# An attention layer over the whole graph: weights divided by their sums beforehand, features on the output's partitions, and one additive term moved to ScalarE

## The chip, the cores and the metric

The kernel runs on one core of a Trainium2 chip. The metric is the device time of one execution in microseconds (us); the runs below give its median and their spread. A profile of one further execution shows what each engine did: TensorE (PE, with its weight loads as PEld), VectorE (DVE), ScalarE (ACT), GpSimd (POOL) and SyncE (SP), which issues the DMAs.

## The reference, cut to what matters

The input x is 32 batches of 512 nodes with 256 features, in fp32. Four graph attention layers follow each other, each as `x = x + layer(relu(layernorm(x)))`. All but a part of the second use an adjacency matrix that is the same for every batch. The second layer holds the part that is changed, an attention over all nodes without a mask:

```python
out = relu(x @ mlp1_w + mlp1_b)            # 512 features
residual = out
h = out @ W_fc                             # relu(out) is out
f1 = h @ a[:F, 0]                          # one score per row i
f2 = h @ a[F:, 0]                          # one score per column j
e = leaky_relu(f1[:, :, None] + f2[:, None, :], 0.2)
out = elu(softmax(e, axis=2) @ h)
out = elu(out) + residual
out = relu(out @ mlp2_w + mlp2_b)          # then a masked attention follows
```

Because the exponential of a leaky rectifier is the larger of two exponentials, an unnormalized weight is the larger of two products, exp(s_i) exp(t_j) and exp(0.2 s_i) exp(0.2 t_j), each shifted by the row's highest score. No exponential over the full 512 x 512 matrix is needed, only products of columns and rows, and a maximum.

## The kernel before, in words

**Tiling.** The nodes of a batch are four tiles of 128 (NT = 4). Features are D = 256 (KD = 2 tiles) or F = 512 (KF = 4 tiles; HF = 256 is half of F). Everything is fp32, apart from masks and throw-away outputs in bf16. `transposes` (line 412) and `product` (line 422) issue all PE work; a product accumulates `nk` matmuls in one PSUM tile.

**Order.** The kernel does not issue work as it is written. Each call of `do` records a piece, with its engine, an estimated duration and the tiles that it reads and writes, in the graph of its batch. `Plan.order` then runs through all graphs, up to five batches being open at once (DEPTH, line 36): it gives each free engine the ready piece with the lowest key, if tiles of its kind are free (SLOTS, line 34). A key is the batch's start (a multiple of PERIOD, line 37) less an entry of the tables URGENCY or FIRST, with corrections for the first and last three batches (EARLY, LAST). Where the plan leaves a gap of 400 ns or more on PE, some filler transposes, `filled`, are put behind the piece (lines 303 to 309 and 1029 to 1031). The instructions stand on each engine in that order, and semaphores keep the dependencies. Tiles come from rings by size: b8 (7 tiles), b4 (14), b2 (14), b1 (10), and 7 PSUM tiles.

**The changed function, `full_gat_T` (lines 841 to 928).** It takes `srcT`, which is out1T, mlp1's output with features on partitions, and overwrites it.

1. The projection: for each half g of the features and each node tile, four matmuls of 257 columns give 256 features of h and one score column. ACT or DVE copies them to `hfc` with 1 added (lines 852 and 854), DVE copies the score (line 855), and POOL writes a column of ones ahead of the first half (line 856).
2. The scores: the highest t of all nodes is found by a reduction, a transpose (`row`, line 861) and another reduction. Then `c` gets four columns per node tile, and one exp of ACT turns them into the factors (lines 867 to 873).
3. The weights: the first factor becomes a row on all partitions by a transpose, a copy (`turned`), a DMA to a line in DRAM and a DMA that broadcasts it (`lines`, `row_of`); the second by four transposes (`spread`). For each node tile jt, ACT scales the one row (line 884) and DVE takes the larger of the two products (line 891) into `ptf`, with the summed-over node j on partitions.
4. The output: for each tile of output nodes and each half, four matmuls with `ptf` as the stationary operand give the numerators, and the first half's extra column gives the denominator. DVE inverts it. ACT applies exp with that scale (line 919), DVE clamps at 1 (line 921), ACT takes exp again (line 922), DVE takes the larger (line 923): the two elu's. The result `ef` has nodes on partitions; 16 transposes per batch bring it back to features on partitions (lines 924 to 926), where DVE adds the residual (line 928).

**The moved term, in `weights_T` (lines 697 to 738).** In two of the four masked attentions of a batch (`even`: after mlp2, and in the last layer), the weights are exp(y + g), where y is the larger of two sums (DVE, line 711) and g is the mask plus a column (POOL, line 717). POOL adds the two (line 721), ACT applies exp (line 722). In the others POOL adds the mask (line 729), and the column is the exp's bias (line 736).

SP issues all DMAs in one order: the batch's input and output, the lines (line 650) and the rows (line 658).

Of the kernel before, what the change touches and what calls it, by code (L numbers as in the profile page):

```python
# [12 lines left out]
AF = mybir.ActivationFunctionType  # L13
# [4 lines left out]
P = 128  # L18
# [18 lines left out]
PERIOD = 103600  # L37
# [7 lines left out]
    43943, 23247, 115444, 28195, 131913, 11021, 150223, 75332, 64495, 133886, 120583, -1101, 94222, 220028,  # L45
    153204, 195513, 90595, 143135, 39950, 165919, 68946, 151319, 9986, 99423, -64152, 52386, 56209, -25494,
    -12505, 125025, -53702, 14840, 134100, 44025, 75158, 8077, 5304, 34581, 45115, 207, -14505, -58518,
    -42176, 75304, -43249, 2933, -19079, -76505, 34586, 51948, 58461, 37338, 44003, -28740, 75374, -78348,
    112017, 44148, -58283, 98931, -23346, -97990, 220212, 87878, 79564, 158375, 51171, 129288, 201256,
    95579, 178029, 176359, -9875, 112826, 199490, -47172, 150423, 84738, 36922, 65744, 89892, 57714, -7531,  # L50
    116483, 40997, 60827, 84702, -240140, 134571, 84185, 72437, 26458, 201340, -116771, -2680, 101206,
    -132113, 11638, 71562, 75236, 19480, 46590, 3896, -69776, 176509, 41349, 41392, 177010, -34515, 59197,
    133037, 87352, 93705, 227861, -7065, 107008, 165322, 17092, 37203, 20572, -3112, 22963, -41216, 38751,
    -37768, 141292, 13106, 30339, 76908, -48735, -54474, 215553, -103644, -6626, 112885, -184359, 72027,
    51563, 88489, 3327, 65551, 105362, 20604, 16381, 36085, 32001, -99329, -107296, -77792, -14723, -136588,
    -100872, -76217, -76147, -259685, -382832, -98027, -197658, -65246, -109857, -125895, -128830, -71459,
    -54813, -57765, 69303, -25676, 10283, -57471, -91828, 79555, 144115, 97457, 180007, 275371, 122987,
    193691, -13364, -53043, -8290, -24035, -15402, -4875, 66615, -8638, -39945, -35041, -48603, -2815,
    -61303, 120173, 102541, 38375, 105200, -71290, -57098, 52007, 94397, -14845, 62753, -26544, -65371,
    -207649, -70898, -69840, -88366, 27159, 104701, 262750, 227584, 196761, 278139, 357683, 279755, 27422,  # L60
    248480, 108362, 230662, 134572, 115371, 155959, 149054, 138805, 77100, 101057, 158810, -88764, 168382,
    77636, 33563, 175809, 112632, 187077, 261718, 117631, 32335, 158631, 1036, -74122, -92596, -12280,
    -146905, 229, 30106, -218718, 7963, -350233, -180610, -79527, -130467, -138492, 17419, -363510, 17356,
    -87268, -271311, -121896, -287651, -76457, -87505, -107851, -318651, -60440, -314406, -66548, -86247,
    -83362, 109349, -288469, 59508, -50249, -21194, -109175, 16924, -42145, -115301, -73511, -299831,
    -68604, -275254, 28335, -37411, -32891, -86918, -129954, -102101, -103415, 21936, -114404, -114436,
    -145621, -54624, -37490, -6786, 226411, -26192, -6061, -25033, 89934, -63272, -82592, 17489, 114806,
    44461, -56264, -87386, -48407, -77170, -87670, -38020, -116914, -38471, -69348, -228506, -215782,
    -54813, -122090, -191577, -55569, -105209, -92182, 28921, -72616, -45523, -49012, -33598, -76273,
    -123170, -174959, 25865, -176706, -124610, -100893, 38989, -172406, -133057, -112099, -99070, -322085,  # L70
    -184282, -219066, -253145, -331833, -169829, -337339, -215940, -163206, -231858, -186736, -108690,
    -196995, -157932, -153450, -248828, -196863, -195477, -223174, -198595, -177361, -206813, -220380,
    -215473, -189492, -160863, -118730, -100154, -74131, 49765, -92141, -214916, -28639, -104791, -137597,
    -30328, -23299, -117546, -70645, -88590, -193216, -218783, -157264, -44754, -117265, -5302, 33583,
    -119484, -41578, 15533, -126430, -111215, -205150, -228722, -168637, -210347, -216720, -159680, -206661,
    -245080, -232690, -61360, -203052, -91590, -122985, -96910, -101903, -107874, -169770, -263511, -226800,
    -253496, -193433, -134757, -250170, -101415, -193028, -330813, -240582, -244977, -358942, -121881,
    -249516, -161367, -68855, -318842, -170307, 33948, -249896, -67102, 38118, -270429, -262193, -234703,
    -182336, -90808, -271458, -194411, -200974, -260557, -213451, -142575, -225302, -284934, -174965,
    -262450, -321002, -146122, -209826, -335580, -243074, -220269, -267185, -269236, -178724, -227851,  # L80
    -396486, -233722, -281737, -132057, -171227, -215236, -199050, -190642, -245900, -181074, -484732,
    -105243, -123637, -227989, -161274, -240673, -150119, -4587, -279569, -211555, -250700, -333147,
    -337122, -257764, -311553, -311455, -273568, -344195, -289986, -197478, -308673, -317223, -455899,
    -303145, -338677, -369201, -488187, -325862, -303656, -344479, -310759, -403328, -446498, -415994,
    -522626, -557538, -378731, -463941, -346054, -453692, -395203, -657915, -481677, -469324, -391813,
    -501282, -465541, -477163, -272939, -582288, -372007, -349639, -208955, -335296, -409233, -455808,
    -447653, -379056, -413166, -439115, -503757, -468515, -418430, -426118, -497159, -360337, -392505,
    -245697, -615652, -650803, -595281,
]
FIRST = [  # L90
    -36661, 19893, -21726, 135503, 85633, 237464, 129132, 171706, 120477, 219412, 125455, 134502, -84836,
    -139537, 39854, 172698, 159381, 199547, 210247, 61158, 103584, 167776, -20431, 3682, 26992, -43725,
    -40836, 27300, 147323, 97757, 40687, 56084, -29470, -69216, -165149, -232111, -89157, -106634, -114869,
    -16735, -130987, 24281, -83920, 52821, -168646, -55535, -145649, -62544, -83048, 6792, -15864, -31602,
    98655, -133287, -166750, -141261, -242450, -135463, -222160, -177245, -98591, -114406, -102410, -79761,
    -264672, -62129, -235867, -253085, -231089, -200529, 16618, -165024, -152414, -165668, 42901, -112970,
    -174603, -113382, -156161, -303346, -252928, -385439, -410003, -195151, -326551, -248605, -317343,
    -163957, -208536, -182534, -24101, -70360, -16833, -208324, -228344, -253210, -209178,
# [3 lines left out]
    [127714, 124300, 140109, 1275316, 20684, 3710, 30790, 20023],  # L102
    [21381, 1446513, 75479, -3218, 89835, 61799, 992, -5994],
    [16582, -743, 947951, -35616, 537487, -26713, 362315, 602],
]
LAST = [
    [136435, 122850, 411901, 1447410, 146100, 513359, -692128, 374735],
    [14763, 42474, 104030, 510068, 166538, -178446, 1731034, 221293],
    [5870, -6330, 13392, 2190, 30176, 62234, 471784, -1052314],
# [226 lines left out]
def gat_stack(  # L336
# [230 lines left out]
    WFC = fixed("wfc", [P, KF, 2, HF + 1])  # L567
# [3 lines left out]
    for s in range(2):  # L571
        for k in range(KF):
            fold(WFC[:, k, s, HF : HF + 1], WFC[:, k, :, :HF], row[:, s])
# [123 lines left out]
    def weights_T(ca, line_b, cc, ct, farT, even):  # L697
# [6 lines left out]
        for jt in range(NT):  # L704
# [8 lines left out]
            if even:  # L713
                g = Later("b2", "g", [P, N])

                def lifted(o, far, c, _):
                    return nc.gpsimd.tensor_scalar(o, far, 1.0, c, ALU.mult, ALU.add)  # L717


                do(POOL, 665, [g.all], [farT[:, jt, :], ct(jt), y.all], lifted)  # L720
# [120 lines left out]
    def full_gat_T(srcT):  # L841

        stt = nc.vector.scalar_tensor_tensor

        hfc = Later("b8", "hfc", [P, NT, 2, HF + 2])
        for g in range(2):
            for t, mm in project(srcT, lambda k: WFC[:, k, g, :], HF + 1, [hfc]):
                v = hfc[:, t, g, 1 : HF + 1]  # L850
                if t % 2 == 0:
                    do(ACT, 300, [v], [mm[:, :HF]], lambda o, a: nc.scalar.activation(o, a, AF.Copy, bias=1.0))
                else:
                    do(DVE, 335, [v], [mm[:, :HF]], lambda o, a: nc.vector.tensor_scalar(o, a, 1.0, None, ALU.add))
                do(DVE, 75, [hfc[:, t, g, HF + 1 :]], [mm[:, HF:]], nc.vector.tensor_copy)
# [21 lines left out]
        for jt in range(NT):  # L877
# [14 lines left out]
            )  # L892


        es = []
        for it in range(NT):
            e = Later("b2", "ef", [P, F])
            rden = Later("tiny", "rdenf", [P, 1])
# [185 lines left out]
```

## Time and profile before

| what | value |
| --- | --- |
| runs, median of 3 | 3432.81 us (3430.71 to 3441.22) |
| profiled execution | 3439.92 us, span of its instructions 3438.2 us |
| mean granted PE clock | 0.996 |
| PE, weight loads | 3400.9, 2852.8 us busy |
| DVE, ACT, POOL | 2678.3, 1965.3, 1640.6 us busy |
| DMA | 110.51 MB, 10.3% of the engines' time in the main queue |
| changed function's product, PE | 2048 records, 489.7 us busy |
| its projection, PE | 2048 records, 471.1 us busy |
| transposes of ef, PE | 512 records, 68.6 us busy |
| the term g, POOL | 256 instructions, 176.6 us busy |

Lines of a group read: source line, engine, operation, output and input tiles, shapes and count; then busy time in us, mean duration of one in ns, and the engine's idle time just before with what ended it. An instruction's row by tile gives shortest, median and longest duration in ns. Lines in order of time give start and duration in us. A wait reads: who waited for whom, us in total, times, longest. An fp32 matmul leaves two records in the profile, a transpose one. PE's records overlap, because a matmul's end is modelled: its busy time is no sum of its means.

### The profile page before, as it was taken

How to read it: one execution, taken by the hardware profiler on the slowest of the kernel's cores; microseconds unless marked ns; L12 is line 12 of the kernel's file. 1: busy time of each engine (PE TensorE's matmuls, PEld its weight loads, DVE VectorE, ACT ScalarE, POOL GpSimd, SP SyncE). 2: the span in 40 equal slices, each digit the busy share in tenths (PEclk: the TensorE clock that was granted, in tenths of full speed). 3: DMA queues.
4: the chain of work that ended last, by engine and by line, in shares of the span. 5: the costliest groups of instructions: out<-in, count | busy, mean ns of one | idle time of the engine just before them, and what ended most of it. 6: DMA issues, size and time to landing. Idle time of an engine off the chain costs nothing. (4 is left out here: it accounts for less than half of the span.)

```text
span 3438.2 us, 55054 instructions
## 1 busy us (share of the span) xinstructions
PE 3400.9 (99%) x18685; PEld 2852.8 (83%) x18685; DVE 2678.3 (78%) x8200; ACT 1965.3 (57%) x4109; POOL 1640.6 (48%) x2089
## 2 busy tenths in 40 slices
PE   8999999999999999999999999999999999999998
PEld 7788888888888888888888888888888888888887
DVE  8587778877878777878778788778788778878675
ACT  3555655665655656555656555656556565556554
POOL 3243544544544535444445445445445354445346
PEclk8999999999999999999999999999999999999999
DMA  3010110011110110100101100101101101001001
GB/s 111 16 32 11 37 38 23 25 35 32 38 38 11 38 35 32 38 26 22 38 28 38 38 26 22 35 32 38 38 12 36 35 32 38 26 22 41 16 23 38
DMA packets 77977, 110.51 MB, mean 32 GB/s; under 512 B 7168, under 2 KB 43520, under 8 KB 77696
## 3 DMA queue, kind: packets, MB, share of 16 engines
q1 hardware_dynamic: 77696, 106.98, 10.3%
q8 instruction: 149, 2.44, 0.3%
q14 instruction: 132, 1.08, 0.1%
HBM read 89.66 MB, written 17.30 MB: 31 GB/s over the span
## 5 line engine op out<-in xcount | busy, mean ns | idle before, releaser
L729 POOL TENSOR_TENSOR y<-y,farT_some 128x512 f32<-128x512 f32 x512 | 579.9, 1162 | 348.9 <-DVE y L711 336.8
L422 PE MATMUL mm<-v,pt 128*128 128x257 f32 x3072 | 704.5, 380 | 2.1 <-ACT pt L722 2.0
L711 DVE SCALAR_TENSOR_TENSOR y<-row,cc,rb 128x512 f32<-128x512 f32 x896 | 619.0, 742 | 59.5 <-DMA rb<-line 37.5
L422 PEld LDWEIGHTS mm<-v,pt 128*128 128x128 f32 x3072 | 573.6, 190 | 85.7 <-ACT pt L722 4.0
L736 ACT ACTIVATE pt<-y,ct 128x512 f32<-128x512 f32 x640 | 457.0, 719 | 171.7 <-POOL y L729 162.1
L422 PEld LDWEIGHTS mmh<-vh,pt 128*128 128x128 f32 x4096 | 489.2, 193 | 11.7 <-issue 1.9
L422 PE MATMUL mmh<-vh,pt 128*128 128x65 f32 x4096 | 485.3, 274 | 1.1 <-ACT pt L736 0.7
L422 PE MATMUL mm<-hfc,ptf 128*128 128x257 f32 (+1 forms) x2048 | 474.1, 381 | 1.2 <-DVE ptf L891 0.9
L422 PE MATMUL mm<-wfc,out1T 128*128 128x257 f32 x2048 | 471.1, 379 | 0.0
L668 DVE CUSTOM_DVE_ANT_0 left<-row,far_nz 128x512 bf16<-128x512 f32 x640 | 414.0, 681 | 64.5 <-PE row L412 64.2
L422 PEld LDWEIGHTS mm<-wfc,out1T 128*128 128x128 f32 x2048 | 382.2, 189 | 53.4
L422 PEld LDWEIGHTS mm<-hfc,ptf 128*128 128x128 f32 x2048 | 379.1, 190 | 52.8 <-POOL y L729 2.2
L721 POOL TENSOR_TENSOR y<-y,g 128x512 f32<-128x512 f32 x256 | 322.4, 1275 | 131.5 <-DVE y L711 116.9
L627 ACT ACTIVATE h<-xt,shift,rstd 128x256 f32<-128x256 f32 x512 | 274.6, 591 | 82.7 <-DVE shift L619 76.6
L612 POOL TENSOR_SCALAR rstd<-mv 128x4 f32<-128x4 f32 x128 | 35.1, 275 | 580.4 <-DVE mv L1028 537.9
L974 POOL TENSOR_TENSOR rz<-rz,res 128x256 f32<-128x256 f32 x128 | 93.7, 733 | 316.2 <-ACT rz L953 310.7
L953 ACT ACTIVATE ez<-mm,rden 128x256 f32<-128x256 f32 x256 | 119.1, 466 | 200.5 <-DVE rden L1028 197.5
L422 PE MATMUL mm<-hT,w 128*128 128x512 f32 x512 | 230.7, 593 | 0.0
L422 PE MATMUL mm<-out1T,wm 128*128 128x512 f32 x512 | 225.2, 592 | 0.0
L1028 DVE BATCH_NORM_STATS2 stats<-xt 128x6 f32<-128x256 f32 x512 | 201.9, 415 | 7.8 <-DMA xt<-in_x_dram 5.0
L668 DVE CUSTOM_DVE_ANT_0 left<-row,far_pos 128x512 bf16<-128x512 f32 x256 | 167.4, 685 | 41.2 <-PE row L412 41.2
L422 PEld LDWEIGHTS mm<-out1T,wm 128*128 128x128 f32 x512 | 95.0, 190 | 107.0 <-issue 99.7
(150 smaller groups left out, 5721.0 us busy)
## 6 DMA issues: line engine op xcount, KB each, us to landing
rb<-line SPq DMA_DIRECT2D x256, 256.0 KB
xt<-in_x_dram SPq DMA_DIRECT2D x32, 512.0 KB
out_dram<-xt SPq DMA_DIRECT2D x32, 512.0 KB
line<-turned SPq DMA_DIRECT2D x128, 2.0 KB
adj_sb<-in_adj_dram SPq DMA_DIRECT2D x1, 1024.0 KB
wfc<-in_L_gnn_W_fc_dram SPq DMA_DIRECT2D x2, 512.0 KB
a_row<-in_L_gnn_a_dram SPq DMA_DIRECT2D x3, 256.0 KB
a_row<-in_L_gnn_a_fc_dram SPq DMA_DIRECT2D x1, 512.0 KB
```

Source lines behind the costliest of these rows:

```text
L422: nc.tensor.matmul(o, lhsT=parts[k], rhs=parts[nk + k], start=(k == 0), stop=(k == nk - 1))
L612: do(POOL, 200, [rstd.all], [mv[:, :, 1]], lambda o, a: nc.gpsimd.tensor_scalar(o, a, EPS, None, ALU.add))
L627: lambda o, a, m, s: nc.scalar.activation(o, a, AF.Relu, bias=m, scale=s),
L668: return nc.vector.tensor_tensor_reduce(out=junk, in0=a, in1=far, scale=1.0, scalar=LOWEST, op0=ALU.add, op1=ALU.max, accum_out=o,)
L711: lambda o, a, c, b: nc.vector.scalar_tensor_tensor(o, a, c, b, ALU.add, ALU.max),
L721: do(POOL, 1255, [y.all], [y.all, g.all], lambda o, y, g: nc.gpsimd.tensor_tensor(o, y, g, ALU.add))
L729: lambda o, y, far: nc.gpsimd.tensor_tensor(o, y, far, ALU.add),
L736: lambda o, a, c: nc.scalar.activation(o, a, AF.Exp, bias=c),
L953: do(ACT, ns, [o.all], [z, scale], lambda o, a, s=scale, f=f: nc.scalar.activation(o, a, f, scale=s))
L974: do(POOL, 685, [r], [r, res[:, it, :]], lambda o, a, b: nc.gpsimd.tensor_tensor(o, a, b, ALU.add))
L1028: made = p.run(*(r.ap() if isinstance(r, Ref) else r for r in p.args))
```

## The change

In `full_gat_T`:

- both score columns are made in the first half of the projection (258 columns), the second has 256; the scores go to a small tile `stf`, and `hfc` has neither ones nor scores;
- the denominators are made before the weights: with output nodes on partitions, ACT scales a row (now the fourth factor), DVE takes the larger of two products and sums it in the same instruction (`accum_out`); the first two factors are multiplied by the inverse sums (`rq`);
- the weights `ptf` are then built as before, from rows and columns of `rq`, so that their sums are 1;
- the product has `hfc` as the stationary and `ptf` as the moving operand, 512 columns wide, with features on the output's partitions; the exps, clamp, maximum and residual follow on 512 columns, without transposes.

In `weights_T`, g is made by ACT (Identity with a bias). All tables of the plan and PERIOD are new.

```diff
-PERIOD = 103600
+PERIOD = 102900
...
-    WFC = fixed("wfc", [P, KF, 2, HF + 1])
+    WFC = fixed("wfc", [P, KF, 2, HF + 2])
...
-            fold(WFC[:, k, s, HF : HF + 1], WFC[:, k, :, :HF], row[:, s])
+            fold(WFC[:, k, 0, HF + s : HF + s + 1], WFC[:, k, :, :HF], row[:, s])
...
-                    return nc.gpsimd.tensor_scalar(o, far, 1.0, c, ALU.mult, ALU.add)
-                do(POOL, 665, [g.all], [farT[:, jt, :], ct(jt), y.all], lifted)
+                    return nc.scalar.activation(o, far, AF.Identity, bias=c)
+                do(ACT, 615, [g.all], [farT[:, jt, :], ct(jt), y.all], lifted)
...
-        hfc = Later("b8", "hfc", [P, NT, 2, HF + 2])
+        hfc = Later("b8", "hfc", [P, NT, F])
+        st = Later("tiny", "stf", [P, 2, NT])
         for g in range(2):
-            for t, mm in project(srcT, lambda k: WFC[:, k, g, :], HF + 1, [hfc]):
-                v = hfc[:, t, g, 1 : HF + 1]
+            n = HF + 2 if g == 0 else HF
+            for t, mm in project(srcT, lambda k: WFC[:, k, g, :n], n, [hfc]):
+                if g == 0:
+                    do(DVE, 75, [st[:, :, t]], [mm[:, HF:]], nc.vector.tensor_copy)
+                v = hfc[:, t, g * HF : (g + 1) * HF]
...
-                do(DVE, 75, [hfc[:, t, g, HF + 1 :]], [mm[:, HF:]], nc.vector.tensor_copy)
-        do(POOL, 80, [hfc[:, :, 0, 0:1]], [], lambda o: nc.gpsimd.memset(o, 1.0))
...
+        low_row = row_of(lines(c[:, 3, :], 1), 0)
+        t_row = spread(lambda t: c[:, 2, t : t + 1])
+        den = Later("tiny", "den", [P, 1, NT])
+        for it in range(NT):
+            low = scaled(low_row, c[:, 1, it : it + 1])
+            do(
+                DVE,
+                740,
+                [den[:, 0, it : it + 1], low],
+                [t_row.all, c[:, 0, it : it + 1]],
+                lambda d, o, a, k: stt(o, a, k, o, ALU.mult, ALU.max, accum_out=d),
+            )
+        rq = Later("tiny", "rq", [P, 2, NT])
+        do(DVE, 80, [den.all], [den.all], nc.vector.reciprocal)
+        do(
+            DVE,
+            78,
+            [rq.all],
+            [c[:, :2, :], den.all],
+            lambda o, a, b: nc.vector.tensor_tensor(o, a, b.to_broadcast([P, 2, NT]), ALU.mult),
+        )
         pt = Later("b8", "ptf", [P, NT, N])
-        r_row = row_of(lines(c[:, 0, :], 1), 0)
-        q_row = spread(lambda t: c[:, 1, t : t + 1], [pt])
+        r_row = row_of(lines(rq[:, 0, :], 1), 0)
+        q_row = spread(lambda t: rq[:, 1, t : t + 1], [pt])
...
-        es = []
-        for it in range(NT):
-            e = Later("b2", "ef", [P, F])
...
-        for f in range(KF):
-            tr = Later("ps", "tr", [P, N])
-            transposes(tr.all, [es[it][:, f * P : (f + 1) * P] for it in range(NT)])
-            o = srcT[:, f, :]
-            do(DVE, 602, [o], [tr.all, o], lambda o, a, b: stt(o, a, -1.0, b, ALU.add, ALU.add))
+        for f in range(KF):
+            e = Later("b2", "ef", [P, N])
+            mm = Later("ps", "mm", [P, N])
+            product(
+                mm.all,
+                [hfc[:, jt, f * P : (f + 1) * P] for jt in range(NT)],
+                [pt[:, jt, :] for jt in range(NT)],
+                N,
+                [e],
+            )
+            z, o = mm.all, e.all
+            do(ACT, 521, [o], [z], lambda o, a: nc.scalar.activation(o, a, AF.Exp, bias=minus1))
+            do(DVE, 335, [o], [o], lambda o, a: nc.vector.tensor_scalar(o, a, 1.0, None, ALU.min))
+            do(ACT, 521, [o], [o], lambda o, a: nc.scalar.activation(o, a, AF.Exp, bias=minus1))
+            do(DVE, 600, [o], [z, o], lambda o, a, b: nc.vector.tensor_tensor(o, a, b, ALU.max))
+            x = srcT[:, f, :]
+            do(DVE, 665, [x], [o, x], lambda o, a, b: stt(o, a, -1.0, b, ALU.add, ALU.add))
```

The new helper `scaled(row, k)` is the ACT scaling of line 884 (Copy with a column as the scale), into a tile `ra`; the weights use it too.

## The prediction

> **What bounds the kernel now.** I read the page's busy times first, then the sum by stretches, then the order of time on PE, to see whether "busy" means work at full pace.
>
> ```profile
> span 3438.2 us, 55054 instructions
> ...
> PE 3400.9 (99%) x18685; PEld 2852.8 (83%) x18685; DVE 2678.3 (78%) x8200; ACT 1965.3 (57%) x4109; POOL 1640.6 (48%) x2089
> ```
>
> ```profile
> core 0: us, PE busy (x) PEld busy (x) DVE busy (x) ACT busy (x) POOL busy (x), PEclk, DMA share, GB/s
> 0.00:40.00 40.00, 26.20 (x196) 25.18 (x196) 31.93 (x90) 12.16 (x22) 5.89 (x17) 0.98 0.65 210
> 40.00:100.00 60.00, 53.70 (x338) 49.88 (x339) 46.78 (x160) 27.75 (x54) 23.49 (x26) 0.81 0.10 30
> ...
> 2200.00:2600.00 400.00, 399.98 (x2167) 333.72 (x2167) 315.96 (x978) 229.45 (x486) 191.48 (x246) 1.00 0.11 33
> 3400.00:3420.00 20.00, 17.51 (x127) 15.65 (x127) 13.52 (x38) 4.37 (x9) 10.42 (x13) 1.00 0.14 32
> 3420.00:3438.20 18.20, 12.28 (x57) 10.06 (x55) 1.17 (x7) 5.98 (x12) 10.88 (x14) 0.91 0.17 58
> ```
>
> In the middle PE lacks 0.02 us of 400; what it lacks lies at the start (20 us in the first 100) and the end (8 us). A rule speaks against trusting this: the Trainium skill (Perfetto Trace Analysis, "Identifying the Most-Contended Engine") calls matmul busy time a bad measure, matmuls being pipelined, and wants the weight loads' share instead. That share is 83%; by it PE has 17% of headroom, something else sets the pace, and fewer matmuls would bring about 0. The order of time decides, by starts and not by ends:
>
> ```profile
> 1011.36 5.37 PE L422 MATMUL mm<-v,pt 128*128 128x257 f32 x24
> 1016.57 0.60 PE L412 MATMUL row<-ident,c 128*128 128x128 f32 x4
> 1017.00 1.25 PE L422 MATMUL mm<-v,pt 128*128 128x257 f32 x5
> ```
>
> ```profile
> 95.85 7.03 PE L422 MATMUL mm<-hT,w 128*128 128x512 f32 x16
> 102.72 1.50 PE L422 MATMUL mm<-w0x,hT 128*128 128x264 f32 x6
> ```
>
> 24 records of 257 columns take 5.21 us, 0.217 each (0.84 ns a column); 16 of 512 take 6.87 us, 0.429 each (the same 0.84); four transposes 0.43 us, 0.109 each. Time follows columns in every shape, with no gap between shapes: PE works back to back, weight loads hide under it, and I cost PE by these spacings (the groups' means of 380 and 593 ns overlap their neighbours).[...]
>
> **The change, part by part.** Counts per run are 32 batches times the loops. PE first, with the rows touched:
>
> ```profile
> L422 PE MATMUL mm<-hfc,ptf 128*128 128x257 f32 x1024 | 244.9, 382 | 1.2 <-DVE ptf L891 0.9
> L422 PE MATMUL mm<-hfc,ptf 128*128 128x256 f32 x1024 | 244.8, 381 | 0.0
> L412 PE MATMUL tr<-ident,ef 128*128 128x128 f32 x512 | 68.6, 275 | 0.0
> ```
>
> - The output comes out with features on partitions, so the transposes of ef go: 512 x 0.109 = -55.8 us.
> - New are one transpose of rq and four for its spread row per batch (the four of c stay): 160 x 0.109 = +17.4.
> - The product's 1024 records at 0.217 and 1024 at 0.216 (443.4) become 1024 of 512 columns at 0.429 (439.3): -4.1. The denominator's column goes, and with it the second width.
> - The projection's 2048 records of 257 become 1024 of 258 and 1024 of 256: 0.
> - Filler transposes: the order of PE's instructions in the two built programs has 381 before and 385 after: +0.4.
>
> Sum -42.1 us, 1.3 us a batch. All of it is on the path, since PE is.
>
> *The other engines* do more, and none becomes the bound:
>
> ```profile
> L919 ACT ACTIVATE ef<-mm,minus,rdenf x256: 542/552/586, 134.5 to 3284.7; 128x256 f32<-128x256 f32 x128
> L921 DVE TENSOR_SCALAR ef<-ef x256: 259/293/1348, 135.1 to 3285.6; 128x256 f32<-128x256 f32 x128
> L922 ACT ACTIVATE ef<-ef,minus x256: 491/498/519, 135.4 to 3286.0; 128x256 f32<-128x256 f32 x128
> L923 DVE SCALAR_TENSOR_TENSOR ef<-mm,rdenf,ef x256: 450/482/485, 135.9 to 3287.1; 128x256 f32<-128x256 f32 x128
> ```
>
> DVE loses L921 and L923 (96.4 + 120.2 busy), L928 (82.4), hfc's column copies (38.7) and rdenf (20.6): 358. It gains 128 each of: the denominator op at 0.745 (nearest L891, same operands; with the 0.083 accumulator read seen at L668 it would be 0.83) 95; the clamp over 512, 0.43 (0.293 plus 256 x 0.54 ns, the slope from L921's shortest, 0.259, to L534's 1.22 over 2048) to 0.60, taken 0.50, 64; the max from PSUM as L711, 0.74, 95; the last add, 0.70 (L962's 0.434 plus L891-L923), 90; stf copies 21; reciprocals and rq 17. That is 382: +24, so 2702 of 3396, 80%. ACT loses 264 and gains 128 rows for the denominator 84 (as L884), 256 exps over 512 at 0.69 and 0.71 (as L944, L736) 179, 256 of g at 0.714 (as L736: bf16 in, pointer bias; near_nz took 0.718) 183, turned 8: +190, 63%. POOL loses g's 176.6 and a memset: 43%. SP gets 32 more lines of 2 KB and 32 more rows of 256 KB, issued in 0.26 and 0.35 us: 20 us of a queue that waits 2703 us for turned.
>
> A rule against it here: the skill (SBUF, "Who interferes with whom") has a DVE op with two SBUF inputs, or a scalar op in its two-port mode, hold the port pair it shares with GpSimd for a whole instruction. The last add changes from PSUM+SBUF to two SBUF inputs and the clamp doubles. By the rule, one POOL add (1.16) before each would cost DVE up to 256 x 1.16 = 297 us: 88%, still below PE. The row: L921's median is 0.293, its mean 0.39, its longest 1.35, so such blocks happen and cost 0.1 on average; I take that.
>
> *Waits.* Latency grows: c, line, row, four denominator ops, rq, and again line, row. What hides it is other batches' PE work. Counting PE's order at the spacings above, the batches in the middle all repeat. Before, 11.4 us of PE work stand between the transpose of c and the first product, and that product waited only 0.9 us for ptf in the whole run:
>
> ```profile
> PE tr L412 <- DVE m_nz L534: 9.7, 1, 9.7
> ...
> PE mm L422 <- DVE ptf L891: 0.9, 2, 0.8
> ```
>
> After, c to rq has 20.6 us over it (that chain plus two or three more DVE ops, some 2.5 us more than the one that 11.4 covered), rq to the first product 15.8 (the old chain): 6.7 and 4.4 to spare. Last product to the mlp2 matmul has 8.8 over 0.69+0.50+0.71+0.74+0.70 = 3.3 us. One cover is thin: tmax to the transpose of c has 2.29, where the exp of c ended 2.40 after tmax in the middle batches; one foreign DVE op of about 0.2 stood inside that chain, and the new order has none. I price it 0 to 0.16 x 32 = 5 us, take 2. With no cover left, each us late costs 32.
> The first of the new ACT scalings waits for its row as L884 does now (idle 51.5 us before it over the run, 1.6 a batch, for rb); behind it in ACT's queue stand exps of weights and copies of PE's results, for which PE waits later. The same again is 51.5 us of ACT idle, within its 37%: 0 where the covers hold, 32 x 1.6 = 51 us if PE had none.
> g on ACT stands in a queue with the exps behind it; each waits 0.71 longer while POOL, relieved of 0.69, has its add ready earlier: 0, and 0.7 x 64 = 45 us if PE had to take it in each of the two gats a batch. The new DMAs' rows wait at SP behind nothing but their own turned; the next gat's rows queue behind them.
>
> *Start and end.* Every due time is new, so both are ordered afresh. Fillers up to the end of the ramp are 196 for 202, after it 189 for 179: no shift that I can count. adj moves behind w0x and a second x (0.75 MB at the 210 GB/s of the first row: +3.7 us), while the first transposes no longer need it. I take 0, between -12 and +12.
>
> The sum against the profiled execution, 3439.9 us (span 3438.2 and 1.7 around it): 3439.9 - 42.1 + 2 = 3399.8. It lay 7.1 above the median of the runs, 3432.8, so against the median: 3392.7, rounded to 3393.
>
> **Rivals.**
> 1. *Part of it eaten* (0.17). The thin cover, or g on ACT, stops PE 0.3 to 0.9 us in each batch. For: ACT +190 us, periodic order, so that a stop repeats 32 times. Against: PE waits of 0.02 us per 400 now. Say 0.65 x 32 = 21: 3414.
> 2. *More saved* (0.06). Start and end, 28 us idle and 41 of fillers, close by 20: 3373.
> 3. *Nothing* (0.03). DVE, at 80%, shares the bound locally, as weight-load share would have it: 3433.
> 4. *Slower* (0.05). The second row comes late: the chain rq, line, row, four weights needs over 15.8 + 1.3 = 17.1 us in every batch, 5.7 more than the 11.4 that suffices now. At that point all the gain is gone; 2.5 us later, 3391 + 32 x 3.8 = 3513; at 0.3 us more, slower by measurement. For: two more rows through one SP queue. Against: SP's idle time.
>
> **How the numbers follow.** The forecast has 0.69, its own range 3378 to 3406 (start and end +-12, thin cover 0 to 5). To leave no more than 2 in 10 out, the upper end reaches into rival 1: 3376 to 3416. Faster is 0.69+0.17+0.06 = 0.92, same 0.03, slower 0.05; under 0.3% (10 us) this kernel's runs, 10.5 us apart, tell nothing.
>
> **What would show it.** Right: no rows tr<-ef; product records 0.429 apart; PE 99% busy with under 1 us missing per 400; one period about 1.3 us shorter in the middle; ACT near 63%, POOL near 43%. Wrong: waits of PE for rq, ptf or c with some 30 entries; the clamp or last add above 1 us; the first 100 us lacking over 32 us of PE. The prediction fails above all if covers counted from one order don't hold in the next.

## The result, and the profile after

| | before | after |
| --- | --- | --- |
| runs, median | 3431.76 us (3430.64 to 3441.22) | 3390.74 us (3388.58 to 3394.96) |
| profiled execution, span | 3439.92, 3438.2 us | 3391.39, 3389.6 us |
| mean granted PE clock | 0.996 | 0.999 |

The ratio is 0.9876, with an interval of 0.9856 to 0.9896: 41.0 us less, where 42.1 - 2 had been forecast. From the page of the changed kernel, the span, the engines' busy times and the costliest group that the change touches:

```profile
span 3389.6 us, 52024 instructions
...
PE 3348.1 (99%) x17313; PEld 2610.8 (77%) x17313; DVE 2732.0 (81%) x8008; ACT 2122.0 (63%) x4269; POOL 1483.5 (44%) x1801
...
L718 POOL TENSOR_TENSOR y<-y,g 128x512 f32<-128x512 f32 x256 | 328.9, 1302 | 243.8 <-ACT g L714 214.3
```

The new chain's instructions, by tile (shortest, median, longest in ns), and g on ACT:

```profile
L932 ACT ACTIVATE ef<-mm,minus x128: 662/687/693, 175.5 to 3261.7; 128x512 f32<-128x512 f32 x128
L933 DVE TENSOR_SCALAR ef<-ef x128: 386/417/1520, 176.2 to 3262.5; 128x512 f32<-128x512 f32 x128
L934 ACT ACTIVATE ef<-ef,minus x128: 701/721/726, 176.7 to 3262.9; 128x512 f32<-128x512 f32 x128
L935 DVE TENSOR_TENSOR ef<-mm,ef x128: 658/685/693, 177.4 to 3263.7; 128x512 f32<-128x512 f32 x128
```

```profile
L714 ACT ACTIVATE g<-farT_pos,ct x128: 704/720/738, 228.8 to 3295.2; 128x512 f32<-128x512 bf16 x128
```

The sum by stretches, in the same columns as before:

```profile
0.00:40.00 40.00, 27.75 (x184) 24.67 (x185) 31.74 (x94) 14.70 (x28) 6.07 (x17) 1.00 0.63 210
40.00:100.00 60.00, 53.47 (x421) 50.02 (x420) 57.03 (x171) 34.44 (x63) 41.95 (x46) 0.97 0.12 37
2200.00:2600.00 400.00, 398.96 (x2053) 310.98 (x2052) 330.07 (x960) 260.44 (x526) 184.27 (x224) 1.00 0.11 35
```

PE still looks full in the middle, yet lacks 1.04 us of 400, more than the 0.02 before, and just over the 1 us that the prediction allowed. The view of waits says where:

```profile
PE tr L409 <- ACT h L624: 17.4, 14, 9.0
```

9.0 us of that is the first instruction of the run (before: 9.7 for m_nz); the other 8.4 is new.

A second measure turned out to be needed: the *period*. In the middle about 23 batches repeat the same sequence of PE instructions, so the time from one batch's first transpose of tmax to the next batch's is one period (the median of 16 is given). *PE's own work* in a period is the sum of its records, each at the spacing that the prediction used. Before, the period was 104.15 us and PE's work 103.53; after, 102.55 and 102.24. By these medians 1.60 us went: 1.29 of work, as forecast, and 0.31 of stalls between starts, which overlapping records hide from the busy time. But the median hides a spread. After, most of the middle's periods last 102.36 to 102.7 us and some up to 105.0; the mean of 22 is 102.97, against 104.34 before. By the mean 1.38 us went, and all but about 0.1 of it is work.

### The profile page after: what moved, and what is told of

Same layout as the page of the kernel before. It is cut to its first block, busy times and chain, and to the rows that moved or that the text cites. A ratio compares the mean times of both kernels' runs of the same rounds, so it can differ in the third digit from the quotient of the medians.

```text
span 3389.6 us, 52024 instructions
## 1 busy us (share of the span) xinstructions
PE 3348.1 (99%) x17313; PEld 2610.8 (77%) x17313; DVE 2732.0 (81%) x8008; ACT 2122.0 (63%) x4269; POOL 1483.5 (44%) x1801
## 5 line engine op out<-in xcount | busy, mean ns | idle before, releaser
L726 POOL TENSOR_TENSOR y<-y,farT_some 128x512 f32<-128x512 f32 x512 | 591.4, 1180 | 375.7 <-DVE y L708 372.9
L708 DVE SCALAR_TENSOR_TENSOR y<-row,cc,rb 128x512 f32<-128x512 f32 x896 | 619.5, 741 | 48.8 <-DMA rb<-line 40.7
L419 PEld LDWEIGHTS mmh<-vh,pt 128*128 128x128 f32 x4096 | 482.7, 192 | 10.2 <-ACT pt L733 3.7
L419 PE MATMUL mm<-wfc,out1T 128*128 128x256 f32 (+1 forms) x2048 | 468.6, 380 | 0.0
L419 PE MATMUL mm<-ptf,hfc 128*128 128x512 f32 x1024 | 456.8, 594 | 0.0
L665 DVE CUSTOM_DVE_ANT_0 left<-row,far_nz 128x512 bf16<-128x512 f32 x640 | 416.3, 683 | 25.0 <-PE row L409 24.4
L419 PEld LDWEIGHTS mm<-ptf,hfc 128*128 128x128 f32 x1024 | 187.9, 190 | 199.9 <-issue 192.1
L726 POOL TENSOR_TENSOR y<-y,farT_self 128x512 f32<-128x512 f32 x128 | 146.2, 1165 | 409.9 <-DVE y L708 402.4
L882 ACT ACTIVATE ra<-rb,c 128x512 f32<-128x512 f32 x256 | 177.6, 715 | 35.1 <-DMA rb<-line 34.9
L854 ACT ACTIVATE hfc<-mm 128x256 f32<-128x256 f32 x128 | 48.4, 378 | 218.0 <-PE mm L419 210.2
```

The lines of the kernel that those rows point to most:

```text
L419: nc.tensor.matmul(o, lhsT=parts[k], rhs=parts[nk + k], start=(k == 0), stop=(k == nk - 1))
L665: return nc.vector.tensor_tensor_reduce(out=junk, in0=a, in1=far, scale=1.0, scalar=LOWEST, op0=ALU.add, op1=ALU.max, accum_out=o,)
L708: lambda o, a, c, b: nc.vector.scalar_tensor_tensor(o, a, c, b, ALU.add, ALU.max),
L726: lambda o, y, far: nc.gpsimd.tensor_tensor(o, y, far, ALU.add),
L882: lambda o, a, k: nc.scalar.activation(o, a, AF.Copy, scale=k),
```

## The experiments

In each, the order of instructions on every engine stays that of its parent, and only what is emitted changes. "Of before" is the ratio to the kernel before on the same chip.

**1. Give the transposes back.** In the changed kernel, four fillers behind each of the four products:

```diff
-            ]
+            ] + [nc.tensor.transpose(filled, ident, ident) for _ in range(extra)]
```

> The changed kernel with four filler transposes behind each of the four products of a batch in the whole-graph attention: 16 x 32 = 512 transposes of 128 columns, as many as the change removed, on PE alone, with no reader; the order on every engine is otherwise that of the changed kernel. Theory (PE works back to back, so time is the sum of its instructions): 512 x 0.109 = +55.8 us, 3390.7 + 55.8 = 3446 (3440 to 3452). Rival (PE is busy only by the records; weight loads at 77% or DVE at 81% set the pace, and the gain came from there): under +10, at most 3401.

Measured: 3446.89 us, 1.0029 of before (1.0018 to 1.0040). The changed kernel on that chip would be 0.9876 x 3438.48 = 3395.8, so 512 transposes cost 51 us there, give or take 8 by the two intervals; 55.8 was forecast. In the new order nearly all work that is added to PE is on the path. That work taken away would pay as fully does not follow from it.

**2. Take them from the kernel before.** One transpose in place of four, its block added four times:

```diff
-            transposes(tr.all, [es[it][:, f * P : (f + 1) * P] for it in range(NT)])
+                lambda o, *parts: nc.tensor.transpose(o[:, 0, :], parts[0], ident),
...
-            do(DVE, 602, [o], [tr.all, o], lambda o, a, b: stt(o, a, -1.0, b, ALU.add, ALU.add))
+                lambda o, a, b: stt(o, a.to_broadcast([P, NT, P]), -1.0, b, ALU.add, ALU.add),
```

> The kernel before with 12 of the 16 transposes of ef per batch left out: of each four only the first is made, and DVE's add of the residual reads that one block four times (so three quarters of the attention's output tiles are not the right ones). Same order on every engine. Theory: 384 x 0.109 = -41.9 us, 3431.8 - 41.9 = 3390 (3384 to 3396), alone nearly the whole gain of the change. Rival (the gain comes from the new order of the start and the end, or from relief of POOL): less than 10 us off, above 3421.

Measured: 3429.77 us, 0.9983 of before (0.9974 to 0.9992): 6 to 9 us (by the ratio and by the medians) for 41.9 us of PE work. The theory fell. The period is 104.14, unchanged, though PE's work in it fell to 102.22. Busy times hardly show that; a stretch of 400 us of this kernel:

```profile
1600.00:2000.00 400.00, 397.80 (x2156) 332.31 (x2155) 318.36 (x983) 234.23 (x493) 191.72 (x244) 1.00 0.10 31
```

PE is 99.5% busy while nearly 2% of each period could go. The order of time, behind the last product of a batch, shows what takes the place (in brackets the idle time before, and what ended it):

```profile
1552.81 7.99 POOL L729 TENSOR_TENSOR y<-y,farT_some 128x512 f32<-128x512 f32 x7 [3.05 <-DVE y L711]
...
1555.24 0.14 PEld L931 LDWEIGHTS tr<-ident,ef 128*128 128x128 f32 x1 [0.39 <-ACT hT L1040]
...
1556.79 0.14 PEld L931 LDWEIGHTS tr<-ident,ef 128*128 128x128 f32 x1 [0.22 <-DVE out1T L939]
...
1557.39 1.14 PE L422 MATMUL mm<-w3x,hT 128*128 128x258 f32 x4 [0.27 <-DVE out1T L939]
...
1558.60 0.72 ACT L736 ACTIVATE pt<-y,ct 128x512 f32<-128x512 f32 x1 [0.40 <-POOL y L729]
...
1559.84 0.73 PEld L422 LDWEIGHTS mm<-w2x,hT 128*128 128x128 f32 x4 [0.41 <-ACT hT L1040]
```

And the same stretch as a sum:

```profile
1551.97:1560.20 8.23, 7.72 (x54) 6.36 (x53) 8.22 (x15) 6.78 (x13) 7.32 (x7) 1.00 0.00 1
```

For 8.23 us DVE is busy 8.22 and POOL 7.32 with seven adds in a row. PE arrives early and waits for DVE's adds of out1T (none of the PE instructions that wait reads out1T: the adds free the PSUM tiles) and for ACT's copies of hT; those copies stand in ACT's queue behind exps that wait for POOL's adds. The theory that followed, tested below: each batch must pass through these few us, DVE's and POOL's work there is fixed, and the transposes lay beside it.

**3 and 4. The move of g alone, in both kernels.** Made on POOL in the changed kernel, at its planned place, and on ACT in the kernel before:

```diff
-                    return nc.scalar.activation(o, far, AF.Identity, bias=c)
+                    return nc.gpsimd.tensor_scalar(o, far, 1.0, c, ALU.mult, ALU.add)
```

> The changed kernel with the term g made by POOL again (the op of before), at the place in the whole order that the plan gave it on ACT; PE's and DVE's orders are unchanged. Theory: the move is worth nothing, since neither engine bounds: 3390.7 (3383 to 3399), with ACT 183 us less busy and POOL 177 more. Rival (relief of POOL is part of the gain): +10 to +25, 3401 to 3416.

> The kernel before with the term g made by ACT, at the place in the whole order that the plan gave it on POOL; PE's and DVE's orders are unchanged. Theory: 3431.8 (3424 to 3440): nothing by itself. Rival (relief of POOL is part of the gain): 10 to 25 us less. A second rival: g behind the queue of ACT comes late, and 64 such waits a batch pair cost 10 to 45 us.

Measured: 3435.32 us, 0.9992 of before (0.9984 to 1.0001), for g on POOL in the changed kernel, so the whole gain is lost; 3436.94, 0.9995 (0.9988 to 1.0002), for g on ACT in the kernel before. The waits of the former:

```profile
ACT h L625 <- DVE shift L617: 203.2, 61, 4.3
...
PE tr L410 <- ACT h L625: 40.0, 54, 9.0
```

PE waits 54 times, not 14, for the normalized h. Counted from a batch's first transpose of tmax (median of 22 batches), g is on POOL from 22.38 to 23.06 us, and all that is queued behind it comes 0.8 us later than in the changed kernel: POOL's first add at 23.57 instead of 22.78, its rstd at 29.96 instead of 29.16, DVE's shift, which needs rstd, at 31.03 instead of 30.22, and ACT's h at 36.36 instead of 35.58. The stall at the transposes of h rises from 0.43 to 1.01 us (means), another of 0.58 follows at those of a later stage, and the period goes from 102.55 to 103.96. An order made for g on POOL might lose less; none was run, so this prices the move in this order.

**5 to 8. Which of the two holds the period.** First both halves of the change in the kernel before; then POOL's adds on 256 of 512 columns:

```diff
-                    lambda o, y, far: nc.gpsimd.tensor_tensor(o, y, far, ALU.add),
+                    lambda o, y, far: nc.gpsimd.tensor_tensor(o[:, :256], y[:, :256], far[:, :256], ALU.add),
```

> The kernel before, in its own order on every engine, with both halves of the change at once: 12 of the 16 transposes of ef per batch are left out (the last add reads the one transposed block four times, so the output isn't the reference's), and g is made on ScalarE instead of GpSimd. Each alone gave nearly nothing (0.9983 and 0.9995 of before). If the two only have to come together, PE's relief and GpSimd's, the time falls by about 40 us, to 0.988. If the period of the kernel before is set by a loop through the fixed orders that passes GpSimd's seven adds of the other kind of stage (those that need no g), then moving g shortens nothing of it and the time stays where the fewer transposes alone left it, 0.997 to 0.999.

> The kernel before with GpSimd's adds of the stage without g made on half of their columns (256 of 512; the second half lacks its mask, so the output isn't the reference's). Same order, same work on PE. If the period of 104.15 us is PE's own work, nothing moves: 0.999 to 1.001. If it is set by a loop through those seven adds (8.0 us in a row), about 4 us of the loop goes away, PE's own 103.53 us becomes the period, and some 0.6 us for each of about 29 batches is saved: 17 us, 0.995.

> The kernel before with 12 of 16 ef transposes a batch left out and with GpSimd's adds of the stage without g on half of their columns; same order; neither output is the reference's. If the loop through the adds is what kept the fewer transposes from paying, the period falls from 104.14 us to PE's 102.22 plus some tenths: 1.6 to 1.9 us for about 29 batches, 46 to 55 us, 0.984 to 0.987. If something else holds the period (VectorE's share, or the weight loads), it stays near 0.998, at best at 0.995 with what the adds give alone.

> The changed kernel with the same adds on half of their columns (the second half lacks its mask, so the output isn't the reference's). Its period is 102.55 us and PE's own work in it 102.24. If PE's work is the bound here, at most 0.3 us for each of about 29 batches can go: between nothing and 9 us, 0.985 to 0.988 of the kernel before. If the loop through the adds still sets the period in the changed order, more than that cannot go either, since PE's work stands below it; a time above 0.988 would say that the shorter adds set off something else.

Measured, of before: 0.9964 (0.9951 to 0.9977), 0.9970 (0.9958 to 0.9982), 0.9942 (0.9927 to 0.9957) and 0.9837 (0.9821 to 0.9854). So the two halves don't simply have to come together in the old order (run 5: 104.14). Run 6 fell between its two forecasts (0.999 to 1.001 and 0.995), and run 7 missed its forecast of 0.984 to 0.987. The periods tell why: half adds give 103.94 with the transposes and 103.94 without them. POOL's adds are one limit, at 104.14; right under it lies another that the transposes don't touch either. In run 8 the adds give 0.4% on top of the change, 10.5 to 14 us (by its own 3380.26 against 3390.74, or against 0.9876 x 3436.86), slightly over what was allowed. The median of its period fell only 0.18 us, to 102.37, but the mean fell 0.34, from 102.97 to 102.62: what went are mostly the stops at the transposes of h, of which 1.6 us are left beside the first instruction's 9.0, where the changed kernel has 8.4:

```profile
PE tr L409 <- ACT h L624: 10.6, 5, 9.0
```

So in the new order, too, what PE still waits for in the middle hangs mostly on POOL's adds.

**9 and 10. The other limit.** Also narrow DVE's last add to 128 of 512 columns, with and without the half adds:

```diff
-                lambda o, a, b: stt(o, a.to_broadcast([P, NT, P]), -1.0, b, ALU.add, ALU.add),
+                lambda o, a, b: stt(o[:, :1], a, -1.0, b[:, :1], ALU.add, ALU.add),
```

> The kernel before with 12 of 16 ef transposes left out, with GpSimd's adds of the stage without g on half of their columns, and now also with VectorE's last add (out1T) on 128 of its 512 columns; the same order on every engine, and the output isn't the reference's. With the transposes gone, the trace shows VectorE busy 8.22 us of the 8.23 us behind the last ef product of a batch, and TensorE waiting there for VectorE's adds and for ScalarE's copies of hT. If VectorE's fixed order in that stretch holds the period, the two adds that come ahead of TensorE's next work lose 0.95 us together, and the period falls from 103.94 to about 103.0 us: 27 us less than with the half adds, near 3389 us, 0.986. If something else holds it, the time stays near 3416, 0.994.

> The same without the half adds: 12 of 16 ef transposes left out, VectorE's last add on 128 of 512 columns, GpSimd's adds whole; the output isn't the reference's. If GpSimd's seven adds, ScalarE's exps that wait for them and the copy of hT behind those hold the period by themselves too, it stays at 104.1 us and the time at 0.998 of before. If VectorE alone holds it, the time falls as with the half adds beside it, to about 0.988 to 0.990.

Measured: 3396.45 us, 0.9878 (0.9863 to 0.9893), and 3427.51 us, 0.9967 (0.9955 to 0.9979). The four kernels without transposes:

| period, us | last add whole | last add narrow |
| --- | --- | --- |
| POOL's adds whole | 104.14 | 104.15 |
| POOL's adds half | 103.94 | 103.17 |

Alone they take 0.20 us and nothing off, together 0.97. With the narrow add alone, PE gets through the adds of out1T early and waits at the next place, for the copy behind POOL's exps:

```profile
1560.75 0.72 ACT L736 ACTIVATE pt<-y,ct 128x512 f32<-128x512 f32 x1 [0.39 <-POOL y L729]
...
1561.38 0.57 ACT L1040 COPY hT<-tr 128x512 f32<-128x512 f32 x1
...
1562.00 0.48 PE L422 MATMUL mm<-w2x,hT 128*128 128x258 f32 x1 [0.81 <-ACT hT L1040]
```

Its waits of PE for that copy are 19.3 us in 24 cases, one a batch. So two chains side by side, DVE's and POOL's, held the period of the kernel before once PE had less to do. At 103.17 there is still 0.95 us over PE's 102.22; 0.56 of it lies at the transposes of ef, behind ACT's copy of hT.

**11 and 12. The covers.** In the changed kernel, four or two more copies in memory on the way of the row of weighted values (the new last argument of `lines`):

```diff
-        r_row = row_of(lines(rq[:, 0, :], 1), 0)
+        r_row = row_of(lines(rq[:, 0, :], 1, 4), 0)
```

> The changed kernel with the line of 1/sum-weighted values taken through four more copies in memory on its way to the spread row: same output, same order on the compute engines. [...]The prediction gave that chain 11.4 us of its own and 15.8 us of TensorE work as cover: if the cover is as worked out, the row is about 4.4 us late in each batch, and the time grows by up to 140 us, to 1.02 to 1.03 of before. If the rest of the order has more room than worked out, or a copy is shorter (1.5 us: 1.6 us late), it grows by less than 50 us. If nothing moves (0.987), the cover was more than twice what the chain needed.

> The changed kernel with two more copies in memory on the way of the row of weighted values (four made it 316 us slower). In the run with four, the row was sent 7.7 us later, so a copy takes 1.9 us and two take 3.8. If the cover is what the prediction worked out, 15.8 us of TensorE work over 11.4 us of chain (4.4 us to spare), two copies fit and the time stays at 0.987. If the place of the scaled rows in ScalarE's own order decides, where four copies left 1.0 us to spare (7.7 late, 6.65 stalled), two stall TensorE by 2.8 us in each of about 29 batches: 80 us, to 1.010; and if TensorE's clock also drops behind so short a gap, as it does behind the long one (3.9 us more in a batch), up to 190 us, 1.04.

Measured: 3706.34 us, 1.0778 of before (1.0760 to 1.0796), and 3533.60 us, 1.0272 (1.0255 to 1.0289): 311 and 136 us over the changed kernel. Both are over what 4.4 us to spare allow. A further copy took 1.8 us, from issue to the next issue. With four, two and no copies the first scaled row starts 14.6, 10.8 and 7.4 us after rq (medians of 32 batches), so 7.2 and 3.4 us late, and PE stops for 5.9 and 2.2 us in each of the middle's periods (medians of 23, of the time between starts that no spacing accounts for). The place, with four:

```profile
1769.53 0.33 PE L419 MATMUL mmh<-vh,pt 128*128 128x65 f32 x2
1771.79 0.72 ACT L893 ACTIVATE ra<-rb,c 128x512 f32<-128x512 f32 x1 [7.45 <-DMA rb<-line]
...
1774.76 0.71 ACT L744 ACTIVATE pt<-y,ct 128x512 f32<-128x512 f32 x1
...
1775.52 1.54 PE L419 MATMUL mmh<-vh,pt 128*128 128x65 f32 x6 [5.65 <-ACT pt L744]
```

PE does not stop at the product that needs the row. It stops 5.2 us of its work earlier (at 33.5 us of the period; in the changed kernel the product starts at 38.7), at a head of another stage (mmh), because an exp for it stands in ACT's queue behind the scaled row. The room was 1.2 to 1.3 us, not 4.4. These stops account for only part of the loss; the last section has the other.

## Why the prediction was right or wrong

**The number** (3393, measured 3390.74; 3399.8 for its own profiled execution, measured 3391.4) was right, within the likeliest case's own range.

**The PE sum, -42.1 us: right as work.** At the same spacings all of PE's records come to 3361.1 us before and 3320.2 after, 40.9 less. Stalls between starts fell from 61.2 to 54.7 us, all of it in the first 100 us (25.3 to 17.8), where the granted clock between 40 and 100 us was 0.81 before and 0.97 after. That is a matter of the execution, not of the new order: the old order lost 17.5 to 22.3 us there in runs 2, 4 to 7, 9 and 10, at 0.89 to 0.94, and the new one 24.4 in run 3, at 0.86. So "start and end", taken as 0 between -12 and +12, stays at about 0 as far as these runs show, and the PE work that went, 40.9 us, by itself matches the 41.0 us between the medians. One reading in it was too wide: time follows columns "in every shape" fails for mmh, whose records of 65 columns start 0.112 us apart where 0.84 ns a column would give 0.055. No term of the sum has that shape.

**"All of it is on the path, since PE is": this step failed, and the number hid it.** It holds in the changed kernel's order, for added work (run 1: 51 of 55.8 us). In the kernel before it was wrong: 41.9 us of transposes taken out gave 6 to 9. That the total came out was luck in this: the new order also moved what held the old one, which the prediction had not asked about. The prediction read "99.98% busy, and starts spaced by columns" as "nothing else limits". Starts so spaced prove that PE works at its pace within a run of matmuls; they don't prove that no loop through other engines is just as long. Before, two loops were as long as PE's own work: one 104.1 and one 103.9 to PE's 103.5 us. The rule on weight loads, weighed and turned down (its section asks for the share of the peak rate beside it, which the prediction left out), had said that fewer matmuls would bring about 0 at a share of 83%; for the old order that was nearer (run 2, share 82%), though for loops, of which it says nothing; for the new order it was far off (run 1: nearly all of the added work counts, with the share at 77% in the changed kernel).

So the gain has three parts that only pay together: less PE work; g off POOL; and a new order with it. Each was left out once: with the transposes given back as fillers the time is 1.0029 of before (run 1), without g off POOL 0.9992 (run 3), without the new order and form 0.9964 (run 5, with 12 of the 16 transposes gone). With all three the period exceeds PE's work by 0.31 us in the median and 0.73 in the mean (before: 0.62 and 0.81). That the missing transposes of ef also free PE from waiting for DVE's and ACT's chain is likely from run 2, where it waits there, but was only argued. How much the new order alone does is open: the old order under the new form, or a new one under the old form, was not run.

**"g on ACT: 0, between 0 and 45": wrong by a sign, and outside the bounds.** It is worth -40 us in the new order (run 3) and 0 in the old (run 4). The prediction named what queues behind g on ACT; it did not ask what queued behind g on POOL, which was four adds and rstd, and behind them shift, h and PE's transposes. The forecast came out since it compared the change as a whole, whose order had the relief in it.

**Waits.** "tmax to the transpose of c, one thin cover, 0 to 5 us" held: the exp of c now ends 1.93 us after tmax, under a cover of 2.28, and PE's waits there don't show. "4.4 us to spare" from rq to the first product failed as a number: runs 11 and 12 put it at 1.2 to 1.3. The step counted PE's work ahead of the product that needs the row, and priced the ACT scalings that wait for it apart, as "0 where the covers hold". The right cover is counted at the first in-order queue where something waits for the row, to the first use of what stands behind it. That ACT itself waits for the other, earlier row of each batch (34.9 us in 32 cases; 51.5 had been allowed) cost PE nothing, as forecast.

**The other engines.** ACT 63% as forecast, POOL 44% instead of 43. DVE came to 2732 instead of 2702. The clamp took 76.1 us instead of 64, the max 87.6 instead of 95, the last add 92.7 instead of 90, the denominator 95.8 instead of 95 (0.75 each, since the accumulator read overlaps the op); together 8 us more. The clamp's block by POOL was the mis-sized term: taken as 0.1 us each, it was 0.18 (mean 595 ns, median 417). Most of the rest is the balance of lines that the change doesn't touch, some longer and some shorter (last section).

**Rivals.** "Part of it eaten": the stop was there at the transposes of h, 0.43 us a period in the mean (about 1.1 in six of 22, next to nothing in half of them), where the old order had 0.28 in every period at its own place; all stalls of the middle together did not grow. "More saved", at start and end: 6.5 us in this pair of executions, by the clock, not by the order. "Nothing": its reason (something other than PE sets the pace) was true of the old order, and would have decided had the change kept that order. "Slower": the second row came in time, but 3.4 us late the changed kernel is 2.7% slower than before, so the point of decision, put at 5.7 us, lies between 1.2 and 3.4.

## What to carry to other kernels

Before costing work off a full engine, compare the period of the repeating part, by median and by mean, with the engine's own work in it: where they differ by a few tenths, look in each stretch for other engines that are full there, since a kernel balanced by a planner has several loops of nearly the same length, and relief of one pays only as far as the next. When an op leaves an engine, list what is queued behind it and follow that to the bound engine; and count the cover of a late transfer at the first queue where an instruction waits for it in order, not at the matmul that uses it.

## What the hardware showed that was not expected

**A gap in PE's work can cost twice.** With four detours, windows of one batch (in the columns as above; the granted clock is the third number from the end):

```profile
1769.00:1776.00 7.00, 1.35 (x8) 1.13 (x7) 1.39 (x6) 4.18 (x9) 2.09 (x3) 0.73 0.16 39
1776.00:1778.00 2.00, 2.00 (x11) 2.00 (x12) 1.12 (x4) 2.00 (x6) 0.98 (x2) 0.50 0.00 0
...
1784.00:1786.00 2.00, 2.00 (x9) 1.64 (x9) 1.04 (x2) 0.75 (x2) 1.16 (x1) 0.55 0.57 198
1786.00:1790.00 4.00, 4.00 (x13) 2.21 (x12) 3.93 (x10) 2.04 (x4) 3.05 (x3) 1.00 0.02 4
```

Behind the gap the clock stays at 0.50 for about 10 us, PE 100% busy all the while; transposes start 0.213 us apart instead of 0.109. Behind every one of 23 gaps of 5.4 to 7.0 us this happened, and behind 10 of the 23 gaps of 1.7 to 3.0 us in the run with two detours, for 6.8 or 10.2 us each. Two stretches of that run, each of about 10 us behind a gap of 2.2 us:

```profile
1270.84:1281.50 10.66, 10.66 (x48) 10.22 (x49) 7.07 (x17) 7.09 (x16) 4.82 (x6) 0.52 0.32 101
1380.20:1391.00 10.80, 9.59 (x58) 7.36 (x59) 9.63 (x23) 8.16 (x18) 6.87 (x8) 1.00 0.32 99
```

The Trainium skill (TensorE: Matmul & The Clock Gate, "What's actually happening") has a free-running window of about 3.4 us that must be idle; the long gaps agree, the 10 short ones, 2.1 to 3.0 us, fell without one. What sets apart the 13 that did not fall, 1.7 to 2.7 us long, these runs don't show. With four detours the slow stretches added 4.7 us a batch to the 5.9 us of the gap.

**A line that was not changed grew by 37 us.** DVE's op on ez has two inputs in SBUF. Before, after, and with POOL's adds halved (run 8):

```profile
L975 DVE SCALAR_TENSOR_TENSOR ez<-ez,rz x128: 401/424/1226, 192.6 to 3347.5; 128x256 f32<-128x256 f32 x128
L984 DVE SCALAR_TENSOR_TENSOR ez<-ez,rz x128: 399/586/1379, 247.6 to 3309.4; 128x256 f32<-128x256 f32 x128
L984 DVE SCALAR_TENSOR_TENSOR ez<-ez,rz x128: 397/418/756, 245.9 to 3297.3; 128x256 f32<-128x256 f32 x128
```

In all it took 54.9 us before, 92.2 after and 64.5 in run 8. In the order of time of the changed kernel:

```profile
909.54 2.28 POOL L726 TENSOR_TENSOR y<-y,farT_some 128x512 f32<-128x512 f32 x2
...
910.73 1.37 DVE L984 SCALAR_TENSOR_TENSOR ez<-ez,rz 128x256 f32<-128x256 f32 x1
```

It starts while POOL's add runs, and ends 0.28 us after it (909.54 + 2.28 = 911.82, against 912.10). So do all the long ones: in the changed kernel 71 of the 128 took over 0.53 us, each of them started while an op of POOL on whole tiles ran, and each ended 0.28 to 0.29 us after it, whether 0.3 or 1.1 us of it had been left. DVE's larger of two sums (L708), which reads one input from PSUM, started 568 of 896 times while POOL was at work and never took over 0.752 us. The port rule that the prediction weighed for the new ops fits this; its price fell mostly on old ops with two inputs in SBUF, which the new order set beside POOL's: 37, 22 and 15 us more on three such lines, while other lines of DVE became shorter by 26, 22, 12 and 12 us.
